# A planned one-core kernel: residual stream moved from TensorE to VectorE, last experts and gate loads rearranged, planner constants retuned

## The chip, the cores and the metric

The kernel runs on one core of one Trainium2 chip. The core has five engines that run side by side, each in the order of its own instruction list, and wait for each other through semaphores: TensorE (PE in the profile; PEld is its weight loading), VectorE (DVE), ScalarE (ACT), GpSimd (POOL) and SyncE (SP), which here only issues DMAs. The metric is the device time of one execution in microseconds (us), lower is better; the figure of a kernel is the median of its runs.

## The reference

Sixteen sequences of 512 tokens with 128 features go through four blocks, each followed by `x = layernorm(x + block(x))`. Cut to what matters:

```python
# 1. RWKV block
x  = ln(x) * ln0_g + ln0_b
xn = ln(x) * pre_g + pre_b ; xx = xn shifted by one token
xk, xv, xr = mixes of xn and xx
k = exp(min(xk @ Wk, 60)) ; v = xv @ Wv ; r = xr @ Wr          # 512 hidden features
wk, wkv = scans over time of k and k*v
x = x + (sigmoid(r) * wkv / wk) @ Wo                           # the time mix is added to the stream
xn = ln(x) * post_g + post_b ; ...
x = x + sigmoid(xr @ cm_Wr) + silu(xk @ cm_Wk) @ cm_Wv         # the channel mix
# 2. soft decision tree: 255 sigmoid gates, 256 leaf probabilities, leaf values, output projection
# 3. causal attention: rms norm, 16 heads of 8, rotary, softmax
# 4. experts: softmax over 16 experts, top 2 kept as gates, every expert computed:
#    u + sum_e gate_e * (u @ W_e + b_e) + mean of two shared experts
```

## The kernel before

All activations lie as 128 features on partitions by 512 tokens, one tile per sequence. A layer norm takes out the mean with a matmul by `centre` (identity minus 1/128); the mean square comes from a matmul with `mean_w`; the reciprocal root is `Ln` and `Exp` on ScalarE (`rstd_of`). float32 matmuls of 512 columns show in the trace as two passes.

The order of the instructions is not written by hand. Each stage is a Python generator, and a planner (`Plan`) runs them against a cost model of the engines, recording an instruction at the moment at which the model finds its engine free and its inputs ready. Pieces that compete for an engine are ranked by a due time: the moment of asking plus a slack from a table for that kind of piece (`S_FRONT`, `S_RWKV`, ... one number for an engine). The result is a fixed list for each engine; on the chip it runs in that order whatever the real durations are.

For each sequence `b`:

- `front(b)` holds the RWKV block, the tree and the attention's projections. Sequence `b` is let in at planner time `PERIOD * b - LEAD`, and not before the time mix of `b-1` was summed. `shifted_norm` makes `xn` (scaled norm, VectorE), `dx` and `xx`; `rwkv(c)` does one of four chunks of 128 hidden features, started `RWKV_PACE` apart.
- `x1` is the stream after the first norm, without its bias. The bias `ln0_b`, centred, is kept as three bfloat16 parts `b0p` and added with a 3-row matmul against `ones`. This is done twice: in `p1` (what the pre norm reads), and in `p2`, where `centre @ x1`, the bias and the four output matmuls of the time mix `tm_o @ rw` are all summed in one PSUM bank. ScalarE then copies `p2` to `x2`; variance and `xn` read the PSUM bank, which is given back only after `xn`.
- `operands` sends rotated q and k through DRAM into three sets of operand tiles (`qop`, `kop`); `greatest` makes scores (`sc`) and their row maxima (`nmx`, VectorE), sends them back as three more operand rows (`rows`, DMA); `weighted` makes the scores again transposed (`st`) and their exponentials `ew` on ScalarE, into a ring of two `e4` tiles of 128x2048 (four head rows by 512); `sums` multiplies them with the values (`o`). Four groups of heads each.
- `ends` normalises, transposes and projects the attention and makes `u`; `gating` makes the top-2 gates and writes them to DRAM (`gT`, then `gd`); then eight DMAs broadcast two experts' gates each to 128 partitions (`gb`, ring of two tiles).
- `by_gate` multiplies `u` with each expert's gate row (`us`, ring of three tiles) on GpSimd; for the last sequence every second one goes to VectorE. `experts` sums `shared` and 16 expert matmuls in the bank `acc`; `output` normalises, transposes and stores.

`V` and `W` are both VectorE; `W` only tells the planner to reckon with a busy GpSimd.

Of the kernel before, what the change touches and what calls it, by code (L numbers as in the profile page):

```python
# [9 lines left out]
F32 = mybir.dt.float32  # L10
# [8 lines left out]
NC4 = 4  # L19
# [21 lines left out]
HAND_OVER = 0.2  # L41
BANKS = 8
SCORES = 5
PERIOD = 100.0

S_FRONT = {"PE": -6.0, "V": -6.0, "A": 0.0, "G": -20.0}
S_RWKV = {"PE": -10.0, "V": 15.0, "A": -10.0, "G": 6.0}
S_GREATEST = {"PE": -30.0, "V": -3.0, "A": -3.0, "G": -30.0}
S_WEIGHTED = {"PE": -20.0, "A": 30.0, "G": -15.0}
S_SUMS = {"PE": 15.0}  # L50
S_ENDS = {"PE": 6.0, "V": -6.0, "A": 50.0, "G": -15.0}
S_GATE = {"PE": -20.0, "V": 6.0, "A": 6.0, "G": 0.0}
S_EXPERTS = {"PE": 20.0}
FREE = {}
LEAD = 60.0
RWKV_PACE = 5.0
EXPERT_PACE = 0.0
MAX_PACE = 0.0
EXP_PACE = 0.0

# [197 lines left out]
def rwkv_tree_attn_moe(ctx: ExitStack, tc: tile.TileContext, a: dict, out: bass.AP):  # L258
# [81 lines left out]
    def col(i):  # L340
        return vec[:, i:i + 1]
# [23 lines left out]
        if scale != 1.0:  # L365
            V.tensor_scalar(w, w, scale, None, ALU.mult)

    ones, b0p, minus = fixed("ones", [PARTS, T], BF16), fixed("b0p", [PARTS, D], BF16), fixed("minus", [128, 2])
    decay, first = fixed("decay", [128, NC4]), fixed("first", [128, NC4])

    def prepare_mixes():

        V.memset(ones, 1.0)
        b0 = pp.tile([128, PARTS], F32, tag="b0", name="b0")
        for i in range(PARTS):
            V.tensor_copy(b0[:, i:i + 1], col(V_LN0B))
        yield
        p = yield from bank("p_b0")
        mm(p[0:PARTS, 0:D], b0, centre, start=True, stop=True)

        act(decay, vec[:, V_DECAY:V_DECAY + 4], AF.Exp)
        act(decay, decay, AF.Exp, scale=-1.0)
        act(first, vec[:, V_FIRST:V_FIRST + 4], AF.Exp)

        V.tensor_scalar(minus[:, 0:1], col(V_PREB), -1.0, None, ALU.mult)
        V.tensor_scalar(minus[:, 1:2], col(V_POSTB), -1.0, None, ALU.mult)
        yield
        b0r = pp.tile([PARTS, D], F32, tag="b0r", name="b0r")
        V.tensor_copy(b0r, p[0:PARTS, 0:D])
        give(p)  # L390
        b0m = pp.tile([PARTS, D], BF16, tag="b0m", name="b0m")
        for i in range(PARTS):
            V.tensor_copy(b0m, b0r)
            V.tensor_tensor(b0r, b0r, b0m, ALU.subtract)
            if i == 0:
                V.tensor_scalar(b0p, b0m, ident[0:PARTS, 0:1], None, ALU.mult)
            else:
                V.scalar_tensor_tensor(b0p, b0m, ident[0:PARTS, i:i + 1], b0p, ALU.mult, ALU.add)
        event("mixes").set()
        yield 12.0  # L400
        centred(tm_o, 0.5)
        centred(cm_v, 0.5)
        event("outputs").set()
# [150 lines left out]
        act(r, r, AF.Exp, scale=-0.5)  # L554
        return r

    def variance(d, tag):

        sq = t512(tag)
        act(sq, d, AF.Square)  # L560
        yield
        pv = yield from bank("pv")
        mm(pv, mean_w, sq, start=True, stop=True)
        yield
        return pv
# [8 lines left out]
    def front(b, keep):  # L574
# [16 lines left out]
        give(p)  # L591
        yield

        def shifted_norm(p, g, minus_b, b):

            r = yield from normed(p, sq, rr)
            shift = yield shifts
            xn = pp.tile([128, T + 1], F32, tag="xn", name="xn")
            G.tensor_copy(xn[:, 0:1], minus_b)
            V.scalar_tensor_tensor(xn[:, 1:T + 1], p, g, r, ALU.mult, ALU.mult)  # L600
            give(p)
            yield
            dx, xx = t512("dx"), t512("xx")
            act(xx, xn[:, 0:T], AF.Identity, bias=b)
            G.tensor_tensor(dx, xn[:, 1:T + 1], xn[:, 0:T], ALU.subtract)
            yield
            return dx, xx, shift
# [5 lines left out]

        yield event("mixes")
        p = yield from bank("p1")
        mm(p, centre, x1, start=True, stop=False)
        mm(p, b0p, ones, start=False, stop=True)
        yield
        dx, xx, shift = yield from shifted_norm(p, col(V_PREG), minus[:, 0:1], col(V_PREB))
        xk, xr, xv = mix(dx, xx, V_MK, "xk"), mix(dx, xx, V_MR, "xr"), mix(dx, xx, V_MV, "xv")  # L620
        shifts.put(shift)
        yield
# [48 lines left out]
        yield event("outputs")  # L671
        yield event("rw", b, 0)
        p = yield from bank("p2")
        mm(p, centre, x1, start=True, stop=False)
        mm(p, b0p, ones, start=False, stop=False)
        event("x1", b).set()
        for c in range(NC4):
            yield event("rw", b, c)
            mm(p, tm_o[:, c, :], rw[:, c, :], start=False, stop=(c == NC4 - 1))
        event("summed", b).set()  # L680
        yield
        if b:
            yield event("rot", b - 1)
        x2 = t512("y")
        copy(x2, p)
        dx, xx, shift = yield from shifted_norm(p, col(V_POSTG), minus[:, 1:2], col(V_POSTB))
        xk, xr = mix(dx, xx, V_CMK, "ck"), mix(dx, xx, V_CMR, "cr")
        shifts.put(shift)
        yield
# [317 lines left out]
    def gating():  # L1007
        yield event("experts")
        for b in range(B):
            yield event("u", b)  # L1010
            keep, u, gaug = kept[b], kept[b]["u"], gaugs[b % 2]
            pl = yield from bank("pl")
            for t in range(NT):
                mm(pl[:, t * NE:(t + 1) * NE], u[:, t * 128:(t + 1) * 128], cent, start=True, stop=True)
            yield

            def small(tag, n=NE):
                return p2.tile([128, NT, n], F32, tag=tag, name=tag)

            def over_e(x):  # L1020
                return x.to_broadcast([128, NT, NE])

            e, m1, m2, s1, s2 = (small(x) for x in ("e", "m1", "m2", "s1", "s2"))
            v1, rs = small("v1", 1), small("rs", 1)
            ranks = rank.unsqueeze(1).to_broadcast([128, NT, NE])
            V.tensor_tensor(e, pl[:, 0:NT * NE].rearrange("p (t e) -> p t e", e=NE),
                            ebias.unsqueeze(1).to_broadcast([128, NT, NE]), ALU.add)
            give(pl)
            V.tensor_reduce(v1, e, AX.X, ALU.max)
            V.tensor_tensor(e, e, over_e(v1), ALU.subtract)  # L1030
            yield
            act(e, e, AF.Exp)
            yield
            V.tensor_reduce(rs, e, AX.X, ALU.add)
            V.reciprocal(rs, rs)
            V.tensor_tensor(e, e, over_e(rs), ALU.mult)

            def first_greatest(x, m, s):

                V.tensor_reduce(v1, x, AX.X, ALU.max)  # L1040
                V.tensor_tensor(m, x, over_e(v1), ALU.is_equal)
                V.tensor_tensor(m, m, ranks, ALU.mult)
                V.tensor_reduce(v1, m, AX.X, ALU.max)
                V.tensor_tensor(s, ranks, over_e(v1), ALU.is_equal)

            first_greatest(e, m1, s1)
            yield
            V.scalar_tensor_tensor(m2, s1, -2.0, e, ALU.mult, ALU.add)
            first_greatest(m2, m1, s2)
            V.tensor_tensor(s1, s1, s2, ALU.add)  # L1050
            gate = gaug[:, :, 0:NE]
            V.tensor_tensor(gate, s1, e, ALU.mult)
            yield
            pg = yield from bank("pg")
            for t in range(NT):
                tr(pg[0:NE, t * 128:(t + 1) * 128], gaug[:, t, :], ident)
            yield
            if b:
                yield event("begun", b - 1)
            gT = pp.tile([NE, T], F32, tag="gT", name="gT")  # L1060
            copy(gT, pg[0:NE, :])
            give(pg)

            gd = dram.tile([NE, T], F32, tag="gd", name="gd")
            nc.sync.dma_start(out=gd, in_=gT)
            yield 3.0
            event("gT", b).set()
            for q in range(NE // 2):
                slot = yield gb_slots
                gb = p2.tile([128, 2, T], F32, tag="gb", name="gb")  # L1070
                nc.sync.dma_start(out=gb, in_=gd[2 * q:2 * q + 2].partition_broadcast(128))
                kept["gb", b, q] = gb, slot
                plan.go(plan.now + 4.0, spread(b, q))
# [6 lines left out]
    def by_gate():  # L1080

        for b in range(B):
            for q in range(NE):
# [1 line left out]
                slot = yield us_slots  # L1085
                gb, slot_gb = kept["gb", b, q // 2]
                us = p3.tile([128, T], F32, tag="us", name="us")
                (W if b == B - 1 and q % 2 else G).tensor_tensor(us, kept[b]["u"], gb[:, q % 2, :], ALU.mult)
                if q % 2:
                    gb_slots.put(slot_gb)  # L1090
                kept["us", b, q] = us, slot
                event("us", b, q).set()
# [1 line left out]
    def experts():  # L1094

        for b in range(B):
            keep = kept[b]
            yield event("gT", b)
            acc = yield from bank("acc")
            mm(acc, shared, keep["u"], start=True, stop=False)  # L1100
            event("begun", b).set()
            for q in range(NE):
# [1 line left out]
                us, slot = kept.pop(("us", b, q))  # L1104
                mm(acc, w_exp[:, q, :], us, start=False, stop=(q == NE - 1))
                us_slots.put(slot)
                if q < NE - 1 and b < B - 1:
                    yield EXPERT_PACE
            yield
            plan.start(plan.now, output(b, acc), S_ENDS)  # L1110
# [79 lines left out]
```

## Time and profile before

| | |
|---|---|
| three runs | 1846.07, 1847.95, 1852.24 us, median 1847.95 |
| the profiled execution | 1852.02 us, span of its instructions 1850.2 us |
| mean granted TensorE clock | 0.957 |
| instructions | 25410 |
| DMA traffic | 133.78 MB |
| `x` of sequence 5, 10, 15 asked for at | 401.5, 901.4, 1420.0 us |
| last exponential `ew` of sequence 15 starts | 1784.5 us |
| last `out` DMA issued | 1847.0 us |

The profile is of one execution. Busy times are sums over instructions of an engine. A matmul's recorded length includes its way through the array, so that neighbours overlap: what a matmul costs TensorE is better read from start to start. The granted clock is the share of full speed that the chip allows TensorE at the time. Names such as `p<-x,centre` are output and inputs of an instruction, buffer numbers left out, so that `p` stands for `p0` to `p3`.

### The profile page before, as it was taken

To read this page: it belongs to the slowest core of one execution; us is meant where nothing else is said; L and a number is where in the kernel's file an instruction comes from. 1 tells how busy PE (TensorE), PEld (TensorE's weight loads), DVE (VectorE), ACT (ScalarE), POOL (GpSimd) and SP (SyncE) were. 2 spreads that over 40 slices of the span, in tenths; PEclk is the share of its full clock that TensorE was granted. 3 is DMA by queue.
4 is the path that set the end of the run, shared out by engine and by line. 5 is a ranking of instruction groups with operands and counts; after the bars stand their busy time and mean duration, and the time that the engine had idled before them with its cause. 6 is when DMAs were issued, how large, how long until landed. Compare 5 with 4: busy or idle time off the path is not lost.

```text
span 1850.2 us, 25410 instructions
## 1 busy us (share of the span) xinstructions
PE 1667.9 (90%) x8580; PEld 784.5 (42%) x8668; DVE 1367.0 (74%) x1917; ACT 1172.0 (63%) x1974; POOL 1063.3 (57%) x1329
## 2 busy tenths in 40 slices
PE   5577889899999999899999999999899999998875
PEld 2233434344444444444444444444344444454431
DVE  7695879688888778686887788796878868555512
ACT  3345677668677576667767676767667666765440
POOL 2344544556765747566565757675666757545342
PEclk9687999899999999999999999999999999999996
DMA  3001010221413122222313132222213131233322
GB/s 103 1 6 56 20 38 27 79 79 32 132 37 112 62 91 78 66 82 73 97 46 105 62 96 78 95 67 65 74 58 116 51 107 62 61 94 111 97 80 97
DMA packets 61970, 133.78 MB, mean 72 GB/s; under 512 B 11708, under 2 KB 32974, under 8 KB 61585
## 3 DMA queue, kind: packets, MB, share of 16 engines
q1 hardware_dynamic: 61841, 132.16, 22.6%
q8 instruction: 69, 1.13, 0.2%
q14 instruction: 60, 0.49, 0.1%
HBM read 114.01 MB, written 17.31 MB: 71 GB/s over the span
## 4 chain that ended last, share of the span: by engine, by line
PE 49%; DVE 25%; POOL 11%; issue 6%; ACT 4%; DMA 2%; SPq 1%; POOLq 0%; DVEq 0%; ACTq 0%
PE acc L219 8%; PE sc L219 7%; PE st L219 6%; DVE sk L219 6%; PE o L219 5%; DVE skv L219 5%; PE p L219 5%; PE pv L219 4%; DVE nmx L219 3%; PE pr L219 2%; PE ph L219 2%; POOL us L219 2%; PE pk L219 2%; POOL lp L219 2%; PE pvv L219 2%
## 5 line engine op out<-in xcount | busy, mean ns | idle before, releaser
L219 DVE TENSOR_REDUCE nmx<-sc 128x1 f32<-128x384 f32 (+3 forms) x704 | 433.8, 634 | 195.6 <-PE sc L219 148.4
L219 ACT ACTIVATE ew<-st 128x512 f32<-128x512 f32 (+1 forms) x704 | 382.3, 556 | 252.1 <-PE st L219 248.0
L219 POOL TENSOR_TENSOR us<-u,gb 128x512 f32<-128x512 f32 x248 | 328.5, 1334 | 159.3 <-PE acc L219 83.6
L219 PE MATMUL acc<-us,w_mo 128*128 128x512 f32 x512 | 277.7, 634 | 17.0 <-POOL us L219 16.7
L219 PE MATMUL st<-qop,kop 128*128 128x512 bf16 (+1 forms) x1018 | 253.9, 304 | 18.1 <-DMA qop<-rows 8.5
L219 PE MATMUL sc<-kop,qop 128*128 128x128 bf16 x1021 | 257.4, 305 | 11.3 <-DVE nmx L219 7.5
L219 DVE RECIPROCAL sk<-sk 128x512 f32<-128x512 f32 x64 | 213.8, 3341 | 0.0
L219 PE MATMUL o<-ew,vaug 128*32 128x512 f32 (+3 forms) x2048 | 193.8, 447 | 6.6 <-ACT ew L219 3.4
L219 POOL TENSOR_TENSOR sk<-fk,sk 128x512 f32<-128x512 f32 x64 | 102.2, 1597 | 142.2 <-DVE sk L219 123.3
L219 PEld LDWEIGHTS <-qop 128*128 128x128 bf16 x1024 | 94.1, 100 | 182.8 <-issue 158.7
L219 PE MATMUL st<-idents,masks 128*128 128x128 bf16 (+2 forms) x673 | 161.7, 240 | 0.6 <-issue 0.4
L219 PE MATMUL sc<-masks,idents 128*128 128x128 bf16 (+2 forms) x656 | 154.9, 236 | 0.3 <-issue 0.2
L219 PEld LDWEIGHTS <-kop 128*128 128x128 bf16 x1024 | 91.6, 99 | 146.7 <-issue 102.5
L219 POOL TENSOR_TENSOR skv<-t,skv 128x512 f32<-128x512 f32 x64 | 81.4, 1272 | 89.1 <-DVE skv L219 84.3
L219 POOL TENSOR_TENSOR rw<-skv,sk 128x512 f32<-128x512 f32 x64 | 86.8, 1357 | 64.5 <-DVE sk L219 61.0
L219 PEld LDWEIGHTS acc<-us,w_mo 128*128 128x128 f32 x512 | 84.1, 195 | 80.7 <-issue 42.1
L219 POOL TENSOR_TENSOR lp<-gates,lp 128x8 f32<-128x8 f32 (+6 forms) x224 | 115.2, 536 | 2.7
L219 DVE TENSOR_TENSOR_SCAN skv<-decay,kv 128x511 f32<-128x511 f32 x64 | 112.7, 1761 | 0.0
L219 PEld LDWEIGHTS <-idents 128*128 128x128 bf16 x704 | 69.8, 99 | 88.8 <-issue 82.9
L219 PE MATMUL pv<-sq,mean_w 128*128 128x512 f32 x160 | 93.2, 666 | 14.3 <-ACT sq L219 13.5
L219 PE MATMUL p<-rw,w_tm 128*128 128x512 f32 x128 | 74.3, 664 | 34.9 <-POOL rw L219 34.5
L219 ACT ACTIVATE r<-pv,eps 128x512 f32<-128x512 f32 x96 | 65.9, 687 | 52.9 <-PE pv L219 30.1
(213 smaller groups left out, 3120.6 us busy)
## 6 DMA issues: line engine op xcount, KB each, us to landing
gb<-gd SPq DMA_DIRECT2D x128, 512.0 KB
qop<-there SPq DMA_DIRECT2D x576, 32.0 KB
kop<-there SPq DMA_DIRECT2D x192, 96.0 KB
there<-parts SPq DMA_DIRECT2D x32, 384.0 KB
x<-xT SPq DMA_DIRECT2D x16, 256.0 KB
out<-sqb SPq DMA_DIRECT2D x16, 256.0 KB
qop<-rows SPq DMA_DIRECT2D x192, 4.0 KB
w_mo<-w_mo SPq DMA_DIRECT2D x1, 1160.0 KB
```

The costliest lines, as they stand in the source:

```text
L219: ins = getattr(self.engine, op)(out, *args, **kw)
```

## The change

1. The stream `x1` becomes a full tensor with its bias: after `p1 = centre @ x1`, ScalarE writes `x1 = p1 + cb0` (Identity with a per-partition bias) back into `x1`, and the bank is given back at once. `cb0` replaces `b0p` and `ones`.
2. `p2` holds only the four output matmuls. VectorE adds `x1` to it while it takes it out of PSUM (`x2`), instead of ScalarE's copy. `shifted_norm` now reads the SBUF tiles `x1` and `x2`.
3. The experts of sequence 14 are recorded only after the last exponential of sequence 15 (`HOLD = 16`).
4. For the last sequence the first four of the eight `gb` loads go into the two `e4` tiles, which are free then, instead of the ring of two.
5. Every second expert multiplication of sequence 14, too, goes to VectorE (`SPLIT = 2`).
6. The planner's constants change: period, lead, paces and most slacks.

```diff
-PERIOD = 100.0
-S_FRONT = {"PE": -6.0, "V": -6.0, "A": 0.0, "G": -20.0}
-S_RWKV = {"PE": -10.0, "V": 15.0, "A": -10.0, "G": 6.0}
-S_GREATEST = {"PE": -30.0, "V": -3.0, "A": -3.0, "G": -30.0}
-S_WEIGHTED = {"PE": -20.0, "A": 30.0, "G": -15.0}
+PERIOD = 96.0
+S_FRONT = {"PE": -6.0, "V": -6.0, "A": 0.0, "G": 0.0}
+S_RWKV = {"PE": -10.0, "V": 20.0, "A": -30.0, "G": 6.0}
+S_GREATEST = {"PE": -30.0, "V": -3.0, "A": 0.0, "G": -3.0}
+S_WEIGHTED = {"PE": -15.0, "A": 3.0, "G": -10.0}
-S_ENDS = {"PE": 6.0, "V": -6.0, "A": 50.0, "G": -15.0}
-S_GATE = {"PE": -20.0, "V": 6.0, "A": 6.0, "G": 0.0}
+S_ENDS = {"PE": 6.0, "V": -3.0, "A": 30.0, "G": -15.0}
+S_GATE = {"PE": -20.0, "V": 6.0, "A": 6.0, "G": 30.0}
-LEAD = 60.0
-RWKV_PACE = 5.0
-EXPERT_PACE = 0.0
+LEAD = 40.0
+RWKV_PACE = 7.0
+HOLD = 16
+HOLD2 = 0
+SPLIT = 2
+EXPERT_PACE = 1.0
...
-            V.scalar_tensor_tensor(xn[:, 1:T + 1], p, g, r, ALU.mult, ALU.mult)
-            give(p)
+            W.scalar_tensor_tensor(xn[:, 1:T + 1], x, g, r, ALU.mult, ALU.mult)
...
         p = yield from bank("p1")
-        mm(p, centre, x1, start=True, stop=False)
-        mm(p, b0p, ones, start=False, stop=True)
-        yield
-        dx, xx, shift = yield from shifted_norm(p, col(V_PREG), minus[:, 0:1], col(V_PREB))
+        mm(p, centre, x1, start=True, stop=True)
+        yield
+        act(x1, p, AF.Identity, bias=cb0)
+        give(p)
+        dx, xx, shift = yield from shifted_norm(x1, col(V_PREG), minus[:, 0:1], col(V_PREB))
...
         p = yield from bank("p2")
-        mm(p, centre, x1, start=True, stop=False)
-        mm(p, b0p, ones, start=False, stop=False)
-        event("x1", b).set()
         for c in range(NC4):
             yield event("rw", b, c)
-            mm(p, tm_o[:, c, :], rw[:, c, :], start=False, stop=(c == NC4 - 1))
-        event("summed", b).set()
+            mm(p, tm_o[:, c, :], rw[:, c, :], start=(c == 0), stop=(c == NC4 - 1))
         yield
         if b:
             yield event("rot", b - 1)
         x2 = t512("y")
-        copy(x2, p)
-        dx, xx, shift = yield from shifted_norm(p, col(V_POSTG), minus[:, 1:2], col(V_POSTB))
+        V.tensor_tensor(x2, p, x1, ALU.add)
+        event("summed", b).set()
+        give(p)
+        dx, xx, shift = yield from shifted_norm(x2, col(V_POSTG), minus[:, 1:2], col(V_POSTB))
...
             for q in range(NE // 2):
-                slot = yield gb_slots
-                gb = p2.tile([128, 2, T], F32, tag="gb", name="gb")
+                if b == B - 1 and q < 4:
+                    slot = None
+                    if q % 2 == 0:
+                        yield e_slots
+                        four = p2.tile([128, HG, T], F32, tag="e4", name="gb")
+                    gb = four[:, 2 * (q % 2):2 * (q % 2) + 2, :]
+                else:
+                    slot = yield gb_slots
+                    gb = p2.tile([128, 2, T], F32, tag="gb", name="gb")
...
-                (W if b == B - 1 and q % 2 else G).tensor_tensor(us, kept[b]["u"], gb[:, q % 2, :], ALU.mult)
+                (W if b >= B - SPLIT and q % 2 else G).tensor_tensor(us, kept[b]["u"], gb[:, q % 2, :], ALU.mult)
...
             yield event("gT", b)
+            hold = {B - 2: HOLD, B - 3: HOLD2}.get(b, 0)
+            if hold:
+                yield event("e", B - 1, (hold - 1) // NT, (hold - 1) % NT)
             acc = yield from bank("acc")
```

More of the change, by code (lines that the diff above doesn't have):

```diff
@@ L366, in centred @@
             V.tensor_scalar(w, w, scale, None, ALU.mult)
-    ones, b0p, minus = fixed("ones", [PARTS, T], BF16), fixed("b0p", [PARTS, D], BF16), fixed("minus", [128, 2])
+    cb0, minus = fixed("cb0", [128, 1]), fixed("minus", [128, 2])
     decay, first = fixed("decay", [128, NC4]), fixed("first", [128, NC4])
     def prepare_mixes():
[L373 to L376, printed above, removed]
-        yield
         p = yield from bank("p_b0")
-        mm(p[0:PARTS, 0:D], b0, centre, start=True, stop=True)
+        mm(p[:, 0:2], centre, vec[:, V_LN0B:V_LN0B + 2], start=True, stop=True)
         act(decay, vec[:, V_DECAY:V_DECAY + 4], AF.Exp)
@@ L387, in prepare_mixes @@
         yield
-        b0r = pp.tile([PARTS, D], F32, tag="b0r", name="b0r")
-        V.tensor_copy(b0r, p[0:PARTS, 0:D])
+        V.tensor_copy(cb0, p[:, 0:1])
         give(p)
[L391 to L398, printed above, removed]
         event("mixes").set()
@@ L555, in rstd_of, with variance @@
         return r
-    def variance(d, tag):
+    def variance(d, tag, bias=0.0):
         sq = t512(tag)
-        act(sq, d, AF.Square)
+        act(sq, d, AF.Square, bias=bias)
         yield
@@ L592, in front, with shifted_norm @@
         yield
-        def shifted_norm(p, g, minus_b, b):
-            r = yield from normed(p, sq, rr)
+        def shifted_norm(x, g, minus_b, b):
+            r = yield from normed(x, sq, rr)
             shift = yield shifts
@@ L1087, in by_gate @@
                 us = p3.tile([128, T], F32, tag="us", name="us")
-                (W if b == B - 1 and q % 2 else G).tensor_tensor(us, kept[b]["u"], gb[:, q % 2, :], ALU.mult)
-                if q % 2:
+                (W if b >= B - SPLIT and q % 2 else G).tensor_tensor(us, kept[b]["u"], gb[:, q % 2, :], ALU.mult)
+                if q % 2 and slot_gb is not None:
                     gb_slots.put(slot_gb)
@@ L1106, in experts @@
                 us_slots.put(slot)
-                if q < NE - 1 and b < B - 1:
+                if EXPERT_PACE and q < NE - 1 and b < B - 1:
                     yield EXPERT_PACE
```

## The prediction

> **What bounds the kernel now.** I read the page's busy rows and slices first, then busy time by stretch of the span, then who TensorE waited for in each stretch, and last the instructions of the end in order of time.
>
> ```profile
> PE 1667.9 (90%) x8580; PEld 784.5 (42%) x8668; DVE 1367.0 (74%) x1917; ACT 1172.0 (63%) x1974; POOL 1063.3 (57%) x1329
> ...
> PE   5577889899999999899999999999899999998875
> ...
> DVE  7695879688888778686887788796878868555512
> ...
> PEclk9687999899999999999999999999999999999996
> ```
>
> TensorE is the engine that is nearly always busy; VectorE has a fifth of its time free until the last fronts are done and half after. The stretches put numbers to it (columns: window, its length, then busy us and instruction counts of PE, PEld, DVE, ACT, POOL, then clock, DMA share, GB/s):
>
> ```profile
> 400.00:1600.00 1200.00, 1154.46 (x6162) 547.07 (x6224) 961.53 (x1309) 832.93 (x1411) 778.31 (x957) 0.99 0.24 76
> 1600.00:1700.00 100.00, 91.92 (x577) 44.97 (x580) 51.57 (x93) 65.31 (x113) 54.09 (x69) 0.98 0.34 102
> 1700.00:1786.00 86.00, 79.72 (x514) 38.97 (x523) 35.26 (x75) 38.62 (x73) 40.52 (x46) 0.98 0.37 115
> 1786.00:1850.00 64.00, 33.26 (x81) 14.01 (x80) 14.69 (x32) 9.56 (x16) 12.84 (x9) 0.71 0.22 74
> ```
>
> From 400 to 1600 us TensorE is idle 45.5 of 1200 us, so a matmul taken away there should shorten the span. The same holds to 1786, where no other engine is over two thirds busy. The first 200 us are not TensorE's: it is busy 129 us, and waits 33.1 us for GpSimd's `rw`. The last 64 us are a chain of single steps: 33 us busy at a clock of 0.71.
>
> **The residual stream.** Counted in the two built programs, 48 matmuls go: 32 of `ones,b0p` and 16 of `x,centre`, three per sequence. Their price from start to start:
>
> ```profile
> 1531.02 1.08 PE L219 MATMUL p<-x,centre 128*128 128x512 f32 x2
> 1532.03 0.39 PE L219 MATMUL p<-ones,b0p 3*128 3x512 bf16 x1
> 1532.34 0.39 PE L219 MATMUL st<-qop,kop 128*128 128x512 bf16 x1
> 1532.57 0.22 PE L219 MATMUL st<-idents,masks 128*128 128x128 bf16 x1
> ```
>
> `centre` takes 1.01 us, a bias matmul 0.31; together 1.63 us a sequence. Part of that is the step between float32 and bfloat16, which stays with the neighbours: with 0.92 (`rw` at 1532.63 to the next at 1533.54) and 0.23 (the `st` above) it would be 1.38. I take 1.5. The first two sequences run while TensorE waits anyway, so 14 x 1.5 = **21 us** less.
>
> What is added lies on other engines.
>
> ```profile
> L219 DVE SCALAR_TENSOR_TENSOR xn<-p,vec,r 128x512 f32<-128x512 f32 x32 | 23.9, 746 | 22.8 <-ACT r L219 22.7
> ...
> L219 DVE SCALAR_TENSOR_TENSOR xk<-dx,vec,xx 128x512 f32<-128x512 f32 x16 | 17.1, 1066 | 14.9 <-POOL dx L219 13.5 <-POOL skv L219 1.4
> ...
> L219 DVE TENSOR_TENSOR att<-z,pw 128x512 f32<-128x512 f32 x16 | 10.7, 666 | 4.1 <-PE pw L219 3.7
> ...
> L219 ACT COPY y<-p 128x512 f32<-128x512 f32 x16 | 9.3, 581 | 17.5 <-PE p L219 17.5
> ```
>
> VectorE gets 16 additions out of PSUM like `att<-z,pw`, 16 x 0.67 = 10.7 us, and its 32 `xn` now read two SBUF tiles, like `xk`: 32 x (1.066 - 0.746) = 10.2 us. That is 1.3 us a sequence on an engine that uses 80 of 100 us. ScalarE changes 16 copies for 16 Identities (0.72 against 0.58, +2.2 us), and the built list has 78 table loads for 74, 4 x 1.28 = 5.1 us; it is 69% busy. The chain of a front grows by some 0.7 us (Identity before the square, slower `xn`), which counts in the first two sequences. I set 2 us for all of it; if the cover failed and VectorE's 21 us came out in full, 21.
>
> Here a rule speaks against the change. The Trainium skill, "SBUF — State Buffer", section "Who interferes with whom", says that a VectorE instruction with two SBUF inputs and a GpSimd one that reads SBUF exclude each other for the whole instruction. The row of the nearest kind says 1.07 us for such an operation, 0.32 more than now, because only part of them meet a GpSimd instruction. By the rule at its worst, each `xn` would stand behind one GpSimd multiplication (1.33 us in the `us` row): 32 x 1.33 = 43 us of VectorE in place of 10, 2.7 a sequence. I take the row: GpSimd is busy 65% of the steady stretch, and `xk` already lives under the same conditions. Even by the rule VectorE would need under 84 of the some 103 us of a sequence.
>
> **The held experts.** In the built order of the old kernel all but three of sequence 14's 17 expert matmuls stand ahead of the last transposed scores of sequence 15; in the new one all 17 stand behind its last `o`. 14 x 0.92 = 13 us leave a stretch that TensorE bounds. But they also covered waits. That stretch shows 5.5 us of waiting for `rows` DMAs (2 waits). Between the last maxima transposes and the first `st` of the last two head groups lay 4.5 and 3.8 us of other TensorE work; now 2.3 and 1.7 (reckoned at the start-to-start times of the trace, 0.22 us for 512 bfloat16 columns and 0.86 for 512 float32 ones), so some 4 us more of such waits appear. Net **-9 us** at the last exponential.
>
> Behind it they stand between the steps of sequence 15's last chain, which before ran with TensorE idle. What is queued behind a late one is the chain itself: `pot`, `ptt`, `pw`, `pv`, `pl`, `pg`. Their gates come through the ring of two, a pair each 2.9 us in the old end (1812.50 to 1833.33, seven steps); 11 experts are ahead of `pl`. Three `us` and three pairs are made before the hold ends, so three more pairs, 8.7 us, are needed in the some 13 us to `pl` (17.5 in the old end from the last `ew`, less the waits named below): it fits. I set +3 us for matmuls standing ahead of chain steps; bounds 0 and 10.
>
> **The last gate loads.**
>
> ```profile
> 1795.76 0.63 ACT L219 ACTIVATE sqb<-att 128x512 f32<-128x512 f32 x1 [2.43 <-DMA out<-sqb]
> ...
> 1796.44 2.07 PE L219 MATMUL pv<-sqb,mean_w 128*128 128x512 f32 x2 [3.73 <-ACT sqb L219]
> ...
> 1812.50 21.15 SPq L1071 DMA_DIRECT2D gb<-gd  x8
> ...
> 1818.20 10.00 PE L219 MATMUL acc<-us,w_mo 128*128 128x512 f32 x16 [6.27 <-POOL us L219]
> ...
> 1839.26 1.98 PE L219 MATMUL acc<-us,w_mo 128*128 128x512 f32 x4 [1.27 <-POOL us L219]
> ```
>
> The eight loads leave one by one as the ring allows; the first `acc` starts 5.7 us after the first issue, the last ends at 1841.2, 23 us later. With six tiles free they need not wait: at an issue every 0.43 us and 1.4 us of transfer each (128 packets of 4 KB on 16 engines, 0.17 us a packet) they land faster than TensorE takes pairs. What is late next is TensorE, 16 x 0.92 = 14.7 us, or GpSimd, 8 x 1.3 to 1.8 = 10 to 14. So 23 becomes 15: -8. Two more go: the wait of `sqb` for the `out` DMA (2.4; that output now comes later), and half-clock steps (`pv` 2.07 against 1.12, `pl` 1.89 against some 1.2, 1.6 together), since held experts keep TensorE busy. Sum -12, with the +3 above **-9 us**. SP issues as many DMAs as before (1249); no `rows` stands behind a gate load of the last sequence.
>
> **The planner's constants** change no work, only order. The new list repeats exactly from sequence 6 to 12; the old one did not. That can gain at most the 45 us of idle time, or repeat a bad wait in each sequence. I take 0.
>
> **Sum:** -21 + 2 - 9 - 9 = -37. From the profiled execution's 1852.0 that is 1815; it ran 4 us over the median of the runs, and from that it is 1811. I say **1812**.
>
> **Rivals.**
> - Only the ends gain (0.24). Steady time is set by chains through VectorE and GpSimd, as the chain that ended last (PE 49%, DVE 25%) hints; the removed matmuls become idle time. TensorE's 3.8% idle speaks against. Then -9 - 9 and a little: 1830 to 1842.
> - The new order also removes waits (0.16): half of the 45 us idle, another -22: 1790.
> - The ends give nothing (0.08): held experts wait on the ring and hold back the chain, 10 us, and eat what the early loads bring: -21 + 2 - 9 + 10 - 9 + 9 = -18, about 1830.
> - Slower (0.14): because the list repeats, one wait that the cost model misjudged is paid in some 13 sequences. The place: VectorE's in-order list, where `xn` and the additions stand ahead of score maxima `nmx`, and TensorE waits for those (6.5 us already from 400 to 1600). Price: a wait of w costs 13w; it decides from 37/13 = 2.8 us a sequence; at the rule's 2.7 us above plus an additional 0.7 for the addition it is 44 - 37 = +7, 1855.
> - No change in effect (0.05): about the same with half of that wait. That the change doesn't do what it says is excluded by the two built programs.
>
> The main case has 0.33, its own range 1800 to 1826. **How the numbers follow:** within 0.3% (5.5 us) is what a measurement can't tell from no change. Faster 0.33 + 0.24 + 0.16 + 0.08 = 0.81, I give 0.80; same 0.06; slower 0.14. The range takes in the better order and most of the half-failed cases: 1785 to 1852.
>
> **What would show it.** Right: TensorE's busy time down some 25 us, busy still over 95% from 400 to 1600, `x` of sequence 15 asked for some 15 to 20 us earlier; the last `ew` near 1755; no TensorE idle over 3 us between the last `ew` and the gate loads; the first six gate loads issued within some 4 us. Wrong: the distance between sequences stays at the 104 us of `x` loads 10 to 15, TensorE's waits for `nmx` or `hid` grow, `xn` is well over 1.1 us, or `pl` of sequence 15 comes more than 18 us after the last `ew`.

## The result and the profile after

The changed kernel takes 1855.07 us (median of 20 runs, 1849.49 to 1863.41), the kernel before, on the same chip, 1848.13 us. The ratio is 1.0038, with a 95% interval of 1.0025 to 1.0051: slower by some 7 us, little more than the 0.3% that can be told from no change. The forecast was 1812. The profiled execution spans 1852.7 us.

The page of the changed kernel, its busy row and the same slices as before:

```profile
PE 1653.8 (89%) x8604; PEld 783.2 (42%) x8604; DVE 1398.1 (75%) x1928; ACT 1180.3 (64%) x1978; POOL 1051.8 (57%) x1321
...
PE   5566789799999999999999999999999999999986
...
DVE  6685969788796868878787978879787978855533
...
PEclk9687989999999999999999999999999999999998
```

TensorE's busy time fell by 14 us, not by 25. (The trace of the kernel before lacks 88 of 8668 matmul records, going by its weight loads, so the true fall may be somewhat larger.) VectorE's rose by 31, which is 10 more than the 21 that were forecast. The same stretches (columns as before):

```profile
400.00:1600.00 1200.00, 1135.13 (x6116) 543.17 (x6113) 975.74 (x1301) 827.40 (x1395) 770.88 (x958) 0.98 0.24 76
1600.00:1700.00 100.00, 94.09 (x570) 46.22 (x569) 61.46 (x115) 64.71 (x112) 54.13 (x71) 0.95 0.28 83
1700.00:1786.00 86.00, 77.68 (x550) 38.38 (x548) 38.10 (x82) 44.13 (x83) 31.54 (x41) 0.96 0.33 107
1786.00:1853.00 67.00, 48.17 (x161) 20.13 (x159) 21.13 (x39) 14.95 (x27) 20.75 (x15) 0.92 0.34 111
```

From 400 to 1600 us TensorE has become busy for less of the time (94.6% against 96.2%), at a lower clock (0.98 against 0.99). In the last window it does twice the matmuls of before at 0.92 instead of 0.71. So the ends are better and the long middle is worse. Milestones say how much:

| us | before | after | moved by | forecast |
|---|---|---|---|---|
| sequence 15's attention input `xa` | 1659.2 | 1679.9 | +20.7 | -21 + 2 = -19 |
| from there to its last `ew` | 125.3 | 112.9 | -12.4 | -9 |
| from there to the end of the span | 65.7 | 59.9 | -5.8 | -9 |

The ends gained 18.2 us, which is what was forecast for them. All of the miss, 40 us, lies ahead of `xa`, in what is repeated for each sequence. (These are single executions: in the run below with all gate loads through the ring, which has the same lists up to there, `xa` comes at 1673.0 us, so 40 is good to some 7.) Who TensorE waited for there, from 400 to 1600 us (total us, times, longest):

```profile
PE pg L222 <- DVE gaug L222: 31.8, 10, 4.0
PE pmx L222 <- POOL nm L222: 16.3, 16, 2.0
```

and the first of them before:

```profile
PE pg L219 <- DVE gaug L219: 3.4, 3, 2.1
```

`pg`, the transposes of the gates, now waits some 3.2 us in each of ten sequences. `gaug` is the last of the small VectorE operations of `gating`, eleven of which read two SBUF tiles. The groups of VectorE by shape, after (busy us, mean ns of one, idle before):

```profile
L222 DVE TENSOR_TENSOR s<-tab,v 128x64 f32<-128x64 f32 x32 | 31.2, 974 | 1.1
L222 DVE TENSOR_TENSOR m<-m,tab 128x64 f32<-128x64 f32 x32 | 28.6, 892 | 1.1
...
L222 DVE SCALAR_TENSOR_TENSOR xn<-x,vec,r 128x512 f32<-128x512 f32 x16 | 13.1, 817 | 12.4 <-ACT r L222 11.8
...
L222 DVE SCALAR_TENSOR_TENSOR xn<-y,vec,r 128x512 f32<-128x512 f32 x16 | 11.9, 745 | 4.2 <-ACT r L222 4.2
...
L222 DVE TENSOR_TENSOR y<-p,x 128x512 f32<-128x512 f32 x16 | 10.9, 684 | 5.2 <-PE p L222 5.2
```

and the first two of them before, with a reduction of as many elements:

```profile
L219 DVE TENSOR_TENSOR s<-tab,v 128x64 f32<-128x64 f32 x32 | 15.7, 489 | 1.1
...
L219 DVE TENSOR_TENSOR m<-m,tab 128x64 f32<-128x64 f32 x32 | 12.0, 375 | 1.1
...
L219 DVE TENSOR_REDUCE v<-m 128x4 f32<-128x64 f32 x48 | 10.6, 220 | 1.7
```

The addition costs what was forecast, and `xn` 1 us more than before instead of 10. What grew most are operations of 64 elements that the change doesn't touch: `s` and `m`, from 0.49 and 0.38 us to 0.97 and 0.89. Other operations of the gating got shorter; the eleven with two SBUF inputs together went from 79.7 to 98.7 us. (The rest of the 31: part 5 brings 6.7 us of expert multiplications to VectorE, and the mixes `xk`, `xr`, `xv`, `ck` and `cr` take 11 us less than before.) The timeline of one sequence of the changed kernel shows why (start, length, engine, operation, idle time before it):

```profile
1187.95 1.26 POOL L222 TENSOR_TENSOR us<-u,gb 128x512 f32<-128x512 f32 x1
...
1188.11 1.19 DVE L222 TENSOR_TENSOR m<-m,tab 128x64 f32<-128x64 f32 x1
...
1188.59 0.27 PE L222 MATMUL st<-idents,masks 128*128 128x256 bf16 x1
1189.17 2.12 POOL L222 TENSOR_TENSOR four<-four,parts 128x1024 f32<-128x1024 f32 x1
1189.33 0.22 DVE L222 TENSOR_REDUCE v<-m 128x4 f32<-128x64 f32 x1
1189.58 1.79 DVE L222 TENSOR_TENSOR s<-tab,v 128x64 f32<-128x64 f32 x1
1191.40 0.23 DVE L222 TENSOR_TENSOR s<-s,s 128x64 f32<-128x64 f32 x1
1191.66 0.23 DVE L222 TENSOR_TENSOR gaug<-s,e 128x64 f32<-128x64 f32 x1
1191.81 0.68 DVE L222 TENSOR_TENSOR y<-p,x 128x512 f32<-128x512 f32 x1
...
1192.04 1.01 PE L222 MATMUL pg<-ident,gaug 128*16 128x128 f32 x4 [3.17 <-DVE gaug L222]
...
1192.84 0.63 PE L222 MATMUL sc<-kop,qop 128*128 128x128 bf16 x4
...
1193.27 0.63 PE L222 MATMUL sc<-masks,idents 128*128 128x512 bf16 x1
```

Read the ends. `m` begins while GpSimd's `us` runs and ends at 1189.30, some 0.1 us after it (1189.21); `s` begins under GpSimd's `four` and ends at 1191.37, again just behind it (1191.29). The reduction between them, with one input, runs its 0.22 us in the middle of `four`, and the next operations of two SBUF inputs, begun after `four`, take 0.23. This is the rule of the Trainium skill that the prediction weighed for `xn` ("SBUF — State Buffer", "Who interferes with whom"); it holds here, on operations that alone take 0.23 us, beside GpSimd instructions of 1.26 and 2.12. Behind them stands the new addition `y`. TensorE stands still for 3.17 us and then runs at half speed: the 512 columns of score matmuls behind it take 0.43 us from start to start, where 0.22 is usual. The clock of that stretch (the number before the last two) falls from 1.00 to 0.55:

```profile
1185.00:1190.00 5.00, 3.79 (x22) 1.17 (x20) 4.69 (x11) 1.95 (x3) 4.03 (x7) 1.00 0.00 0
1190.00:1195.00 5.00, 2.96 (x17) 2.00 (x18) 3.11 (x5) 2.20 (x5) 1.29 (x1) 0.55 0.01 2
```

The timeline of the end of the changed kernel:

```profile
1800.92 0.63 ACT L222 ACTIVATE sqb<-att 128x512 f32<-128x512 f32 x1 [1.94 <-DVE att L222]
...
1801.71 1.02 PE L222 MATMUL pv<-sqb,mean_w 128*128 128x512 f32 x2
...
1819.86 3.22 SPq L1065 DMA_DIRECT2D gb<-gd  x6
...
1825.91 12.00 PE L222 MATMUL acc<-us,w_mo 128*128 128x512 f32 x24 [1.34 <-POOL us L222]
...
1834.72 2.05 SPq L1065 DMA_DIRECT2D gb<-gd  x2
...
1840.38 3.74 PE L222 MATMUL acc<-us,w_mo 128*128 128x512 f32 x8 [2.46 <-POOL us L222]
```

Six loads leave within 3.2 us, as forecast, and `sqb` no longer waits for the `out` DMA. But the last two still wait for the ring, 15 us behind the first, and TensorE waits 2.46 us for what they bring: 18.2 us from the first `acc` to the last where 15 were forecast.

### The profile page after: what moved, and what is told of

It reads as the page before. It is cut to its first block, busy times and chain, and to the rows that moved or that the text cites. A ratio compares the mean times of both kernels' runs of the same rounds, so it can differ in the third digit from the quotient of the medians.

```text
span 1852.7 us, 25314 instructions
## 1 busy us (share of the span) xinstructions
PE 1653.8 (89%) x8604; PEld 783.2 (42%) x8604; DVE 1398.1 (75%) x1928; ACT 1180.3 (64%) x1978; POOL 1051.8 (57%) x1321
## 4 chain that ended last, share of the span: by engine, by line
PE 52%; DVE 25%; POOL 10%; issue 4%; DMA 4%; ACT 4%; SPq 1%; DVEq 0%; POOLq 0%; ACTq 0%
PE sc L222 8%; PE acc L222 8%; DVE skv L222 7%; PE p L222 7%; PE st L222 6%; PE o L222 5%; PE pv L222 5%; DVE sk L222 4%; POOL us L222 3%; DVE nmx L222 3%; DMA gb<-gd 3%; PE ph L222 2%; PE pr L222 2%; PE pvv L222 2%; DVE m L222 2%
## 5 line engine op out<-in xcount | busy, mean ns | idle before, releaser
L222 DVE TENSOR_REDUCE nmx<-sc 128x1 f32<-128x384 f32 (+3 forms) x704 | 438.7, 636 | 183.2 <-PE sc L222 180.4
L222 POOL TENSOR_TENSOR us<-u,gb 128x512 f32<-128x512 f32 x240 | 315.6, 1322 | 203.9 <-PE acc L222 113.9
L222 PE MATMUL acc<-us,w_mo 128*128 128x512 f32 x512 | 266.5, 616 | 13.0 <-POOL us L222 10.2
L222 PE MATMUL st<-qop,kop 128*128 128x512 bf16 (+3 forms) x1024 | 257.6, 307 | 16.5 <-DMA qop<-rows 13.3
L222 PE MATMUL sc<-kop,qop 128*128 128x128 bf16 (+3 forms) x1024 | 262.5, 310 | 0.2
L222 PE MATMUL sc<-masks,idents 128*128 128x128 bf16 (+2 forms) x704 | 176.6, 251 | 0.0
L222 PE MATMUL st<-idents,masks 128*128 128x128 bf16 (+2 forms) x704 | 175.0, 249 | 0.0
L222 POOL TENSOR_TENSOR lp<-gates,lp 128x8 f32<-128x8 f32 (+6 forms) x224 | 119.4, 555 | 1.9
L222 PE MATMUL pv<-sq,mean_w 128*128 128x512 f32 x160 | 97.4, 694 | 15.3 <-ACT sq L222 14.4
L222 POOL TENSOR_TENSOR dx<-xn 128x512 f32<-128x512 f32 x32 | 33.1, 1035 | 133.6 <-DVE xn L222 133.6
```

What stands on the lines that cost most here:

```text
L222: ins = getattr(self.engine, op)(out, *args, **kw)
```

## The experiments

Times are read as ratios to the kernel before, run beside each; 0.001 is 1.85 us. A replanned kernel gets another order everywhere, so most of these keep the lists of each engine as they were: the planner is charged for what is removed, and an instruction is replaced by one at its place.

**Is the wait of `pg` the cost, or only the first to show it?** In the changed kernel, same lists, the transposes read the gates of the sequence before:

```diff
-                tr(pg[...], gaug[:, t, :], ident)
+                tr(pg[...], (gaugs[(b + 1) % 2] if b else gaug)[:, t, :], ident)
```

> The changed kernel with the same instruction list on every engine; only the four transposes pg read the gates of the sequence before instead of their own (the output is therefore another one), so that they need not wait for gaug. Theory A (one wait repeated in each sequence, with the half clock that follows it, ate the gain): in the changed kernel pg waits 3.17 us in about 11 sequences and each wait is followed by 3.4 to 6.8 us of half clock, so 11 x (3.17 + 1.7 to 3.4) = 54 to 72 us at most, some of it taken back by later waits: 1800 to 1820 us, the distance between sequences near 101 us instead of 104.9. Rival B (the distance is set by VectorE and GpSimd, pg only shows it): another wait takes its place, 1845 to 1855 us, distance 104 to 105.

Measured: 1856.66 us, 1.0039 (1.0020 to 1.0059), the time of the changed kernel. TensorE's waits from 400 to 1600 us:

```profile
PE sc L222 <- DVE y L222: 18.9, 8, 2.4
PE pmx L222 <- POOL nm L222: 15.6, 14, 2.6
```

The wait for `gaug` is gone, and the score matmuls behind it wait for `y`, the addition, which stands behind `gaug` on VectorE. It is VectorE that is late; `pg` was merely its first customer.

The other way to spare that wait records `pg` later (`yield` becomes `yield 7.0` ahead of it), which replans everything:

> The changed kernel, but the planner lets the gate transposes pg be recorded 7 us after the last gating step, so that other TensorE work stands ahead of them; the whole order changes with it and no longer repeats. Theory A: pg waits gone or under 1 us, 1810 to 1830 us. Rival B: 1845 to 1860 us, as other waits take its place.

Measured: 1872.08 us, 1.0124 (1.0099 to 1.0148), above both expectations. The largest wait is now for ScalarE's `sq` (18.4 us from 400 to 1600). Another order, another wait: it says nothing of `pg`.

**The ends.** `HOLD = 0`, same lists up to the ends:

> The changed kernel without the hold on sequence 14's experts; the lists are the same up to the last two sequences. If the hold works as forecast (13 us of TensorE work out of the stretch before the last exponential, some of it paid back): 6 to 12 us slower than the changed kernel, the last exponential about 10 us later. Rival (held experts only delay the last chain): no difference or faster by up to 5 us.

Measured: 1867.7 us, 1.0094 (1.0064 to 1.0123). The hold of the experts is worth 0.0056, or 10 us, give or take 6.

All gate loads through the ring (`if False:` in place of `if b == B - 1 and q < 4:`):

> The changed kernel with all eight last gate loads through the ring of two; the lists differ in the last few rows. By the forecast 8 us slower (last expert matmuls over 23 us instead of 15). By the trace of the changed kernel, where the last two loads still wait for the ring, 3 to 4 us slower. Rival: no difference, TensorE or GpSimd sets the pace anyway.

Measured: 1859.9 us, 1.0062 (1.0040 to 1.0085). The early loads are worth 0.0024, or 4 us, half of what was forecast, but with some 5 us either way. The trace agrees with it: from the first of the last `acc` to the end of them it takes 23.5 us here, 18.2 in the changed kernel.

**What are the 48 matmuls worth?** The kernel before without them, same lists (its sums lack the bias and, in `p2`, the stream):

```diff
-        mm(p, centre, x1, start=True, stop=False)
-        mm(p, b0p, ones, start=False, stop=True)
+        mm(p, centre, x1, start=True, stop=True)
+        plan.did("PE", 0.02 + 0.0004 * T)
...
-        mm(p, centre, x1, start=True, stop=False)
-        mm(p, b0p, ones, start=False, stop=False)
+        plan.did("PE", 0.0018 * T)
+        plan.did("PE", 0.02 + 0.0004 * T)
...
```

> The kernel before with the same lists on every engine, only the 48 matmuls (32 bias, 16 centre in p2) are left out, so that the bias and the stream are missing from the sums. By the forecast's first term (TensorE bounds the steady stretch): 21 us faster than before, some 1827 us. Rival (the in-order lists of TensorE and VectorE hold each other, and TensorE's freed time turns into waiting): 0 to 8 us faster, 1840 to 1848 us.

Measured: 1841.79 us, 0.9937 (0.9918 to 0.9956), 12 us less instead of 21, between the two expectations. From 400 to 1550 us (1150 us less TensorE's busy time there) its idle time rose from 42.9 to 55.0 us: over half of what was taken away turned into waiting.

**What does the work that came in cost?** The whole stream edit (parts 1 and 2 of the change) in the kernel before, at its order: `aside` puts an instruction at the place of the last one of its engine, `x2` is VectorE's addition at the place where ScalarE's copy stood. The PSUM banks are given back after `xn`, as before, not at once.

```diff
+        aside("A", nc.scalar.activation, x1, p, AF.Identity, bias=cb0)
...
-        copy(x2, p)
+        plan.did("A", 0.2 + 0.00078 * T)
+        aside("V", nc.vector.tensor_tensor, x2, p, x1, ALU.add)
```

> The kernel before with the stream's whole edit (48 matmuls less, x1 with its bias by ScalarE, addition and xn from SBUF on VectorE) put into the old lists: the planner is charged as before, so every other instruction keeps its place. By the forecast (-21 + 2): 1829 us. By the run without the matmuls (-10) and hidden work on VectorE: 1840 to 1845 us. If VectorE's added 1.3 us a sequence come out: 1855 to 1865 us.

Measured: 1856.62 us, 1.0033 (1.0020 to 1.0047). Against the run before it, the added work costs 0.0096, or 18 us. Here `xn` does take 1.0 us, by shape:

```profile
L219 DVE SCALAR_TENSOR_TENSOR xn<-y,vec,r 128x512 f32<-128x512 f32 x16 | 16.4, 1023 | 7.5 <-ACT r L219 7.5
L219 DVE SCALAR_TENSOR_TENSOR xn<-x,vec,r 128x512 f32<-128x512 f32 x16 | 15.9, 997 | 12.2 <-ACT r L219 12.0
```

**What does GpSimd's hold on the gating cost?** (The hold here is VectorE kept waiting by GpSimd, not `HOLD`.) In the changed kernel, same lists, ten of the eleven small operations with two SBUF inputs of each sequence become reductions over an axis of one, with one input (`alone`), so the gates are others; only the subtraction `e<-e,v` keeps its two:

```diff
-                V.tensor_tensor(m, m, ranks, ALU.mult)
+                alone(m, m)
```

> The changed kernel with the same lists on every engine; eleven of the small gating operations of each sequence on VectorE are made reductions over an axis of one with one SBUF input (the gates are therefore other numbers), so that GpSimd's rotary multiplications can't hold them. Theory C (GpSimd holds these operations in each sequence, gating takes 12 us for 7.6, and VectorE is late for pg, for the addition of x1 and for the score banks): gating under 9 us, pg waits under 1 us, distance between sequences 101 us, 1800 to 1825 us. Rival (the next wait takes its place again): distance 104 to 105 us, 1843 to 1855 us.

Measured: 1800.22 us, 0.9719 (0.9686 to 0.9752). The same substitution in the kernel before:

> The kernel before with the same lists, its small gating operations made one-input as in the changed kernel's run (the gates are therefore other numbers). In before gating takes 8.6 to 12.5 us, unevenly, and pg waited 3.4 us in all of the steady stretch. If the hold by GpSimd cost before little: 0 to 15 us faster, 1835 to 1850 us. If it cost before as much as the changed kernel: 45 to 55 us faster, 1795 to 1805 us.

Measured: 1814.89 us, 0.9811 (0.9786 to 0.9836). The hold costs the kernel before 35 us too, though its trace shows 3.4 us of waits for `gaug`; that lies between the two expectations. And without it the change is worth 0.0092, or 17 us.

The same in a form that computes all: the operands stay, but `e`, `m1`, `m2`, `s2` and `v2` live in the PSUM bank that the logits `pl` came in, so that each operation has one input in SBUF at most:

```diff
-            e, m1, m2, s1, s2 = (small(x) for x in ("e", "m1", "m2", "s1", "s2"))
+            e, m1, m2, s2 = (pl[:, NT * NE * i:NT * NE * (i + 1)].rearrange("p (t e) -> p t e", e=NE) for i in range(1, 5))
+            s1, v2 = small("s1"), pl[:, 5 * NT * NE:5 * NT * NE + NT].unsqueeze(2)
...
-            give(pl)
...
+            give(pl)
```

> The changed kernel with the same lists on every engine and the full computation; the gating's small tiles are kept in the PSUM bank of the router scores, so that no small operation has two SBUF inputs (the bank is given back after the gates are made). Theory C: as with one-input forms, gating under 9 us, 1797 to 1810 us, ratio to before 0.970 to 0.980. Rival (the one-input run gained by something else, as its other numbers): 1845 to 1856 us.

Measured: **1799.9 us, 0.9715 (0.9699 to 0.9732)**, the fastest of all that ran, with the work of the changed kernel. The two groups that had grown, by shape, and the middle stretch:

```profile
L222 DVE TENSOR_TENSOR pl<-pl,v 128x64 f32<-128x64 f32 x48 | 11.1, 232 | 1.6
...
L222 DVE TENSOR_TENSOR pl<-pl,tab 128x64 f32<-128x64 f32 x32 | 7.4, 232 | 1.1
```

```profile
400.00:1600.00 1200.00, 1154.75 (x6316) 556.34 (x6383) 954.06 (x1357) 859.37 (x1448) 793.68 (x980) 1.00 0.27 80
```

An operation takes 0.23 us, the clock is 1.00, and in the same 1200 us TensorE completes 200 matmul records more. Its `xa` of sequence 15 comes at 1625.8, 54.1 us earlier than in the changed kernel, and its end 54.6 earlier: the whole gain lies in the repeated stretch.

**With the hold gone, what are the parts worth?** The less-matmuls kernel and the stream kernel, each with `alone` in the gating:

> The kernel before without the 48 matmuls (bias and stream missing) and with one-input gating (other gates), same lists. If the hold halved the worth of the matmuls: 1792 to 1797 us, 18 to 23 below the 1815 of one-input gating alone. If the in-order lists halve it in any case: 1803 to 1808 us.

> The same with the small gating operations made one-input (other gates). Against the kernel before with one-input gating (1815 us): if VectorE's added work is hidden once GpSimd holds less, 1795 to 1806 us; if it comes out, 1815 to 1830 us.

Measured: 1806.31 us, 0.9750 (0.9732 to 0.9768), and 1816.3 us, 0.9802 (0.9784 to 0.9820). Against the kernel before with `alone`, the matmuls are worth 0.0061 (11 us); against the run without them, the added work costs 0.0052 (10 us).

**Other orders.** The changed kernel with the constants of before; the stream edit alone, replanned; the kernel before with the new constants; and the changed kernel whose planner reckons the gating operations as slow (`W` for `V`):

> The changed kernel (stream, hold, last gate loads, split) with the planner constants of before. If the new constants and the order that they make ate the gain: 1810 to 1835 us. If the order matters little and the stream brings nothing: 1845 to 1860 us.

> The kernel before with the stream's edits alone (x1 with its bias, addition by VectorE), constants of before, no hold, ring for all gate loads, no second split. By the forecast's terms for the stream (-21 + 2): 1829 us. If it brings nothing or costs (VectorE's added 1.3 us a sequence stand in the way): 1848 to 1860 us.

> The kernel before with the new planner constants alone. If the constants are good by themselves: 1820 to 1845 us. If they fit only the changed stream, whose order they make periodic: 1850 to 1890 us.

> The changed kernel, but the planner reckons with a busy GpSimd for the small gating operations; its order no longer repeats. If knowing of the hold is enough: 1805 to 1830 us. If an uneven order costs as much as in the other replanned runs: 1850 to 1880 us.

Measured: 1880.87 us, 1.0155 (1.0123 to 1.0187); 1893.39, 1.0228 (1.0196 to 1.0260); 1872.51, 1.0115 (1.0096 to 1.0134); 1863.41, 1.0064 (1.0047 to 1.0080). None is faster than the changed kernel, and only the last one's interval meets that of the changed kernel. The first two lie above both of their expectations. The constants of either kernel do badly with the other's work, but delaying a single piece (`yield 7.0` above) cost nearly as much. So these runs don't show whether constants and work fit each other or most new orders cost something; neither can be judged by a run that replans.

## Why the prediction was wrong

The parts by the ratios, in us (1850 times the difference). The work was priced at the order of before. With GpSimd's hold, the order's share is what remains; without it, ends and order were measured together. Part 5, which the prediction doesn't price, was not run alone and is in the order's share.

| part | forecast | as the kernels are | no hold on the gating |
|---|---|---|---|
| 48 matmuls away | -21 | -12 | -11 |
| work added on VectorE and ScalarE | +2 | +18 | +10 |
| ends (hold 10, early loads 4) | -18 | -15 | together -15 |
| new order | 0 | +16 (remainder) | |
| sum | -37 | +7 | -17 |

By the intervals a single entry is good to some 4 to 6 us, the ends together, the remainder and the last column's sum to some 8.

1. **"A matmul taken away there should shorten the span"** failed in its size: -12 for -21. The 1.5 us a sequence were taken off TensorE, but in a fixed order it then waits for partners that come no earlier: its idle time rose by 12 us (from 400 to 1600 us it waited 9.8 us for GpSimd's `nm` instead of 7.0, and 7.7 for `nmx` instead of 6.5). That it was busy 96% of the stretch did not show that it set the pace alone.
2. **"I set 2 us for all of it"** is one of the two terms that failed worst: +18. The cover was named as a VectorE that uses 80 of 100 us. That is an average. In the changed kernel the addition stands at one place of an in-order list, behind `gaug`, and the run with other gates showed TensorE's `sc` waiting for it there. The prediction's own end value, 21 if the cover failed, was nearly right. How much of the 18 falls in the changed kernel's own order was not measured; `xn`, 1.0 us in the old order, is shorter there.
3. **The rule, weighed only for `xn`.** The prediction took the row (1.07 us) over the rule for `xn`. In the changed kernel `xn` takes 0.75 to 0.82, so there even the row was dear, and in the old order 1.0. But the rule also holds for every other VectorE operation with two SBUF inputs, and the rows of `s` and `m`, with means of 489 and 375 ns for 64 elements beside 220 for a reduction of as many, showed before the change that it bit there. The prediction does not use them.
4. **"The planner's constants change no work, only order ... I take 0"** failed: +16, by what remains. The sentence before it, that the order can "repeat a bad wait in each sequence", is what happened. The new lists put `gating` under GpSimd's `four` and `us` each time: from the first `e<-pl` to the end of `gaug` it takes 12.0 us in every sequence from 4 to 12, before 8.6 to 12.2 (median 9.0), with PSUM operands 7.4. The 19 us that the eleven operations grew by are of the size of the +16. Taking the hold away gains 60 us in the changed kernel by the ratios, 43 in the stream edit at the old order, 35 before. Without the hold the new order costs nothing that can be measured: ends and order together give -15, as the ends alone do with it, each good to some 8 us.
5. **The held experts**: -9 forecast, -10 measured, give or take 6. Right.
6. **The last gate loads**: "they need not wait" holds for six of eight; -8 was some -4. The waits of `sqb` and the half clock of `pv` went, as said. (A pair's step in the old end is 20.83/7 = 3.0 us, not 2.9, and the 4 KB packets of that stretch took 0.16 us in the median and 0.19 on average, where 0.17 was taken; nothing hangs on either.)
7. **The rivals.** Slower, at 0.14, was the outcome. Its kind was right: a misjudged wait paid in each sequence. It decides "from 2.8 us a sequence"; the 40 us missing at `xa` are 3.1 in each of 13. Its place was wrong: not `xn` ahead of `nmx` (TensorE's waits for `nmx` stay small), but the gating ahead of `pg` and of the next `x2`. So it is luck that its number, 1855, is the measured one. Of what was to show the main case wrong, the distance of the `x` loads from sequence 10 to 15 did: 104.8 us, before 103.7. Of what was to show it right, only the two signs of the end came: no idle time of TensorE over 2.73 us between the last `ew` and the gate loads, and six loads within 3.2 us.

How the hold reaches TensorE in the changed kernel, from 400 to 1550 us: idle 63.5 us, with PSUM operands 43.3; at half clock 47.8 us against 3.4, which at half speed is up to 22 us of work lost. The two together, 20 + 22, are most of the 55 us between the medians. For the kernel before this doesn't come out: with `alone` its idle time falls from 42.9 to 27.1 us and its half clock from 20.5 to 6.8, together 23 of 35 us.

VectorE's own sums come nearer. The eleven operations with two SBUF inputs take 39.9 us in all with PSUM operands, 98.7 in the changed kernel: 59 us less work on VectorE gained 60. With `alone` they fall from 79.7 to 41.6 us before and from 79.6 to 41.6 in the stream edit: 38 us less gained 35 and 43. So the time taken off these operations came out about one for one, on an engine that is busy some 80% of the steady stretch, while the matmuls off TensorE at 96%, priced at 21, gave 12. This is a match of three sums, not a mechanism; why it is one for one is open, and so is why the added work costs 18 us with the hold and 10 without it, since the two differ by little more than their intervals.

## What to carry to other kernels

A small VectorE operation beside a busy GpSimd should not read two SBUF tiles: look for groups whose mean is several times that of a like-sized operation, and move one operand to PSUM; here that was worth eight times what the whole change cost. The busy share does not say which engine's time counts: price a part by an experiment that removes it. With fixed lists, free time of an engine is no cover on average: ask what stands behind the new instruction at its place, and when a wait is removed, which instruction asks next for the same late engine. To price a part where a planner orders the work, keep the lists and change the instruction; the stream edit alone took 1.0033 at the old order and 1.0228 replanned, 36 us apart.

## What the hardware showed

The hold was known as a rule; its size was not expected: operations of 0.23 us took up to 2.06 (`gaug` at 556.97 us of the changed kernel), and eleven of them in a sequence cost 3% of the kernel.

Short waits were enough to halve TensorE's clock. In the changed kernel each of the eight waits of 3.17 us from 770 to 1510 us comes with 3.4 or 6.8 us of half clock. In the sequence shown it lasts from 1190.5 to 1197.4 us: it begins 1.7 us after the last `st` ended (1188.86), while TensorE still stands idle. Shorter gaps do it too: in the run with other gates seven of eight gaps of 2.37 us are followed by half clock, and in the kernel before a gap of 1.97 us (1482.83 to 1484.79, half clock from 1485.83 to 1489.24). The Trainium skill ("TensorE: Matmul & The Clock Gate", "HAM oscillation — how this bites in real kernels") puts the limit at gaps over some 3.4 us; here gaps of 2.0 to 3.2 us did it, and the measurement decides.
